# A decoder layer on one core: queries and keys projected without padding and spread by DMA, maxima by one transpose, scores by four or two heads, the projections' chain in two

## The chip, the core and the metric

The kernel runs on one core of a Trainium2 chip. A core has five engines that run their own instruction lists in order and meet only at semaphores: TensorE (PE in the profile; its weight loads are PEld), VectorE (DVE), ScalarE (ACT), GpSimd (POOL) and SyncE (SP), which here does nothing but issue DMAs. The metric is the time of one execution on the device in microseconds (us), the median of several runs.

## The reference

One layer, three sub-blocks, each followed by `x = layernorm(x + ...)`: a selective scan (a state-space block) whose state starts anew every 64 tokens, a cross attention of 16 heads of 16 columns to a given context, and a gated FFN in which each token belongs to one of eight experts by its position. Batch 32, 256 tokens, width 256, all in 32-bit floats.

```python
xc, res = jnp.split(x @ W_in.T + b_in, 2, axis=-1)          # 512 each
u = silu(conv(xc) + conv_b)                                  # causal, 3 taps
dlt, Bm, Cm = jnp.split(u @ W_x.T, [64, 80], axis=-1)
delta = softplus(dlt @ W_dt.T + b_dt)
dA = exp(einsum('bld,dn->bldn', delta, -exp(A_log)))
dBu = einsum('bld,bln,bld->bldn', delta, Bm, u)
carry = a * carry + bu ; y = einsum('bkdn,bkn->bkd', carry, c)
out1 = (y * silu(res)) @ W_out.T + b_out
...
q = proj(x, w_q, b_q) ; k = proj(ctx, w_k, b_k) ; v = proj(ctx, w_v, b_v)
attn = softmax(einsum('bhqd,bhkd->bhqk', q, k) / 4)
out2 = einsum('bhqk,bhkd->bhqd', attn, v) @ w_o.T + b_o
...
out3 = einsum('becf,efd->becd', silu(x @ w1) * (x @ w3), w2)
```

## The kernel before

**An order made by a planner.** `decoder_kernel` describes the work as chains, Python generators that yield the planned time and the engine of their next step. `in_order` (L78) keeps a planned clock per engine, always takes the chain that can go on first (ties by the chain's lag, the second argument in L1090 to L1104), and writes its instructions down. That order is final: on the chip each engine runs its list as written. The planner's durations are constants (`MM`, `EV`, `VE`, `GP` and numbers inside `spend`); a DMA counts as landed `LANDING` = 4.5 us after its step, and SP's own time is not counted, since no step spends on SP.

**Buffers.** PSUM has a ring of six banks for all products (`RING`, `take`, `done`, `bank`): a chain asks for n banks with a rank, and a step with a higher rank number waits while one with a lower asks.

**The scan** (`scan`, `decays`, `weighted`, `sums`). A batch has 16 steps of 32 channels by 16 states. SP loads delta and delta*u of step i+3, two DMAs that repeat rows over the states (`load_step`, L485), into one of four buffers; ScalarE makes the decays (four instructions, L519), in one of three buffers; VectorE multiplies (L544) and scans (L563), two of each; GpSimd multiplies by C (L580); after every four steps TensorE sums over the states (L594) and frees four of six state buffers.

**What feeds it** (`pre`, one chain for the whole of a batch): transpose x, project, convolve, `Silu` into `u` (L398, one buffer), then L408 on the product with `w_x`, the copy to DRAM (`bcd`, L422), delta through softplus on ScalarE and GpSimd, and two writes to DRAM (`dd`, L460 and L465) that the next batch's `load_step`s read. The small term of the softplus goes in two halves of two channel blocks (`lost`, L445 to L452).

**The attention** (`keys`, `attn`, `finish`). The host pads each head of `w_q`, `w_k` and their biases from 16 to 32 columns, so that four heads fill 128 partitions and each lies at a multiple of 32. The keys' bias holds 1.0 in the padded row 16 of each head. A padded projection is 512 columns: two `product`s of four matmuls (L626 to L638, L693 to L703), each copied with its bias by ScalarE (`biased`, L333) into `kT` and `qT`. Chain `keys` for batch b+1 starts after the last sum of batch b (`attended`), and `attn` takes one batch after the other.

In `attn` the first pass makes scores for four heads at a time (L715, four banks), and VectorE takes the maximum over keys (L731) into row 16 of each head's block of `mpad`. Eight 128x128 transposes (L739) turn `mpad`, and VectorE subtracts the result from `qT` (L742), which puts minus the maximum into row 16 of each head; its product with the keys' row of ones subtracts the maximum from the scores in the second pass. That pass makes the scores transposed, again four heads at a time, exponentiates them (`es`, L775) and multiplies by `v` with a column of ones (L751).

**The FFN** (`expert_unit`, `fetches`) runs in the gaps once a group of batches is stored, two units at a time at the end; the second set of units borrows the scan's buffers by tag.

All DMAs of the kernel are issued by SP. At the start it issues all weights, then 64 DMAs of `a_neg`, and `load_x(0)` last (L1088).

Of the kernel before, what the change touches and what calls it, by code (L numbers as in the profile page):

```python
# [95 lines left out]
def decoder_kernel(ctx: ExitStack, tc: tile.TileContext, a: dict, out: bass.AP):  # L96
# [54 lines left out]
    def row(name):  # L151
        t = wp.tile([P, D], F32, name=name)
        nc.sync.dma_start(t, a[name].partition_broadcast(P))
        return t

    w_in = weight("w_in", D, 2 * DI)
    b_in = column("b_in", 2 * NDC)
# [27 lines left out]
    b_out = row("b_out")  # L185
    w_k = weight("w_k", D, NG * P)
    b_k = column("b_k", NG)
    w_v = weight("w_v", D, D)
    w_out = weight("w_out", DI, D)
    w_q = weight("w_q", D, NG * P)  # L190
    b_q = column("b_q", NG)
    w_o = weight("w_o", D, D)
# [56 lines left out]

    mpad = keep.tile([P, 2, NG, P], F32, name="mpad")  # L250
    nc.gpsimd.memset(mpad, 0.0)

# [3 lines left out]
    def take(n, rank, t):  # L256
# [12 lines left out]
        del free[:n]  # L269

    def done(n, t):
        free.extend(n * [t])
# [12 lines left out]

    MM = 0.43
    EV = {1: 0.47, 2: 0.6, 4: 1.06}
# [49 lines left out]

    xs_at, xps, dds, sress, bcds, ygs, spread, silus = {}, {}, {}, {}, {}, {}, {}, []
    gated, stored = {}, []

    def exps():

        nc.scalar.preload_act_table_set("natural_log_exp_and_others")
        spend("ACT", 1.28)

    def pre(b):
# [50 lines left out]
        spend("ACT", 1.28)  # L397
        u = unit1.tile([P, NDC, L], F32, tag="u", name=f"u_{b}")  # L398
        for c2 in range(2):
            t = biased(u, AF.Silu, conv_b, pss[c2], c2)  # L400
            done(1, t)
        nc.scalar.activation(sres, sres, AF.Silu)
        spend("ACT", EV[4])
        sress[b] = sres
        while silus:
            silus.pop(0)()
        exps()
        yield from take(1, 3, t)  # L408
        ps = bank("ps_x")[:, :L]
# [34 lines left out]
        yield spend("ACT", EV[4]), "POOL"  # L444
        for h in range(2):  # L445
            cc = slice(2 * h, 2 * h + 2)

            lost = unit1.tile([P, 2, L], F32, tag="xT", name=f"lost_{b}")
            nc.gpsimd.tensor_scalar(lost, e[:, cc], 1.0, -1.0, op0=ALU.add, op1=ALU.add)
            nc.gpsimd.tensor_tensor(lost, e[:, cc], lost, ALU.subtract)  # L450
            nc.gpsimd.tensor_tensor(z[:, cc], z[:, cc], lost, ALU.add)
            yield spend("POOL", 3 * GP[2]), "POOL" if h == 0 else "ACT"  # L452
        nc.scalar.activation(e, e, AF.Ln, bias=1.0)
# [11 lines left out]
        nc.sync.dma_start(dds[b][1].rearrange("(c p) t -> p c t", p=P), u)  # L465
        spread[b] = t + 3.0

    def pres():
        for b in range(B):
            yield from pre(b)  # L470
        while silus:
            silus.pop(0)()
# [54 lines left out]
    def scan():  # L527
# [4 lines left out]
        for i in range(STEPS):  # L532
# [6 lines left out]
            for g in range(GB):  # L539

                if g:
                    yield t - 0.3 - MARGIN, "DVE"
                bu = ps_bu.tile([P, NQ, L], F32, tag="bu", name="bu")
                nc.vector.tensor_tensor(  # L544
                    bu, loads[i][:, 1, g].unsqueeze(1).to_broadcast([P, NQ, L]), b_bc, ALU.mult
                )
                t = spend("DVE", 0.66)
                if g == GB - 1:
                    del loads[i]
                    if k == NBLK - 1 and b + 1 < B:  # L550
                        yield t, "PE"
                        spread_b(b + 1)
                t -= 0.3 + MARGIN
                if g == 0:
                    yield lambda: (
                        max(t, decayed[i], min(h_free)) if i in decayed and h_free else None
                    ), "DVE"
                    h_free.sort()
                    del h_free[0]
                    h = hs[i] = hp.tile([P, GB, NQ, L], F32, tag="h", name="h")  # L560
                else:
                    yield t, "DVE"
                nc.vector.tensor_tensor_scan(  # L563
                    h[:, g].rearrange("p q t -> p (q t)"),
                    das_of[i][:, g].rearrange("p q t -> p (q t)"),
                    bu.rearrange("p q t -> p (q t)"),
                    0.0,
                    op0=ALU.mult,
                    op1=ALU.add,
                )  # L570
                t = spend("DVE", 1.17)
            del das_of[i]
# [10 lines left out]
    def sums():  # L583


        for i in range(NJ - 1, STEPS, NJ):
# [4 lines left out]
            for g in range(GB):  # L591
                for q in range(NQ):
                    for j in range(NJ):
# [8 lines left out]
                        )  # L602
            t = spend("PE", GB * NQ * MM + 0.3)
            h_free.extend(NJ * [t])
# [12 lines left out]
    kts, x1Ts, attended, oSs, ending = {}, {}, [], [], []  # L617

    def keys():

        for b in range(B):
# [3 lines left out]
            ctxT = cts.pop(b)  # L625
            kT = unit1.tile([P, NG, L], F32, tag="kT", name=f"kT_{b}")  # L626
            for g2 in range(2):
                yield from take(1, 4, t0)
                ps, t = product(
                    "ps_qk",  # L630
                    lambda j: [
                        w_k[:, k, (2 * g2 + j) * P : (2 * g2 + j + 1) * P] for k in range(2)
                    ],
                    lambda j: [ctxT[:, k, :] for k in range(2)],
                )
                yield t, "ACT"
                t = biased(kT, AF.Identity, b_k, ps, g2)
                done(1, t)  # L638
            yield from take(1, 4, t0)
# [8 lines left out]
            done(1, t)  # L648
            kts[b] = kT, t

# [38 lines left out]
    def attn(b):  # L689

        yield lambda: x1Ts[b][1] if b in x1Ts else None, "PE"
        x1, (x1T, tx) = x1s.pop(b), x1Ts[b]
        qT = unit1.tile([P, NG, L], F32, tag="qT", name=f"qT_{b}")  # L693
        for g2 in range(2):
            yield from take(1, 2, tx)
            ps, t = product(
                "ps_qk",
                lambda j: [w_q[:, k, (2 * g2 + j) * P : (2 * g2 + j + 1) * P] for k in range(2)],
                lambda j: [x1T[:, k, :] for k in range(2)],
            )  # L700
            yield t, "ACT"
            tq = biased(qT, AF.Identity, b_q, ps, g2)
            done(1, tq)  # L703
        del x1Ts[b]
        yield lambda: max(tq, kts[b][1]) if b in kts else None, "PE"
        kT = kts.pop(b)[0]

        def scores(g, left, right):


            ss = [bank("s").rearrange("p (t n) -> p t n", t=2) for _ in range(4)]
            for t in range(2):
                for j in range(4):
                    r = 32 * j
                    nc.tensor.matmul(  # L715
                        ss[j][:, t, :],
                        left[r : r + 32, g, t * P : (t + 1) * P],
                        right[r : r + 32, g, :],
                        start=True,
                        stop=True,  # L720
                    )
            return ss, spend("PE", 2 * MM + 0.5)


        t = tq
        for g in range(NG):
            yield from take(4, 2, tq)
            ss, ts = scores(g, qT, kT)
            for j, s in enumerate(ss):
                yield ts, "DVE"  # L730
                nc.vector.tensor_reduce(mpad[:, :, g, 32 * j + DK], s, AX.X, ALU.max)  # L731
                t = spend("DVE", VE[2])
                done(1, t)
        for g2 in range(2):
            yield from take(1, 2, t)
            ps = bank("ps_m").rearrange("p (j t n) -> p j t n", j=2, t=2)
            for j in range(2):
                for n in range(2):
                    nc.tensor.transpose(ps[:, j, n, :], mpad[:, n, 2 * g2 + j, :], ident)  # L739
            yield spend("PE", 0.6), "DVE"  # L740
            q2 = qT[:, 2 * g2 : 2 * g2 + 2, :]
            nc.vector.tensor_tensor(q2, q2, ps.rearrange("p j t n -> p j (t n)"), ALU.subtract)  # L742
            tq = spend("DVE", VE[2])
            done(1, tq)

        def attend(g, ess):

            oT = bank("ps_oT")[:, :L]
            for k in range(2):
                for j in range(4):  # L750
# [8 lines left out]
                    )  # L759
            return oT, spend("PE", 2 * MM + 0.3)  # L760

        last, oS, te = None, None, 0.0
        for g in range(NG + 1):
            if g < NG:
                yield from take(4, 2, tq)
                ss, ts = scores(g, kT, qT)
            if g:
                yield from take(1, 0, te)
                oT, to = attend(g - 1, last)
            if g < NG:  # L770
                ess = []
                for s in ss:
# [5 lines left out]
                    done(1, te)  # L778
                last = ess
            else:  # L780
                attended.append(to)
# [84 lines left out]
    class Buffers:  # L866
# [18 lines left out]
        def h(self, u, n):  # L885

            m = 2 * L // n
            if self.own:
                t = unit1.tile([P, 3 * m, n], F32, tag="h_ff", name=f"h_{u}")
                return [t[:, b * m : b * m + m, :] for b in range(3)]  # L890
            return [
                unit1.tile([P, m, n], F32, tag=tag, name=f"h_{tag}_{u}")
                for tag in ("u", "delta", "e")
            ]
# [182 lines left out]
    def units(bufs):  # L1077
# [19 lines left out]
        Chain(finishes(), -3.0),  # L1097
        Chain(pres(), 1.0),
        Chain(keys(), 1.5),
    ]  # L1100
# [69 lines left out]
```

## Time and profile before

| | us |
|---|---|
| median of 3 runs (lowest, highest) | 3283.39 (3279.27, 3285.63) |
| the profiled execution | 3283.71 |
| its span, first to last instruction | 3282.0 |

| engine | busy us | share of the span | instructions |
|---|---|---|---|
| PE | 2697.9 | 82% | 18436 |
| PEld | 1907.2 | 58% | 18436 |
| DVE | 2584.0 | 79% | 3511 |
| ACT | 1970.8 | 60% | 4211 |
| POOL | 1857.3 | 57% | 1241 |

The mean granted TensorE clock is 0.897, and DMA queue 1, which is SP's, holds the 16 DMA engines busy 47.8% of the span. The first scan runs at 119.8 us, the last loads of the scan are issued at 2962.7, and from 3100 to 3282 VectorE works 33 us of 182: FFN is left there. A row of the profile that names one line of a helper (L327 is in `product`, L333 in `biased`) is told apart by its tiles. In a row of the groups, the columns are line, engine, operation, out<-in, shapes and count, then busy time and mean ns of one, then the idle time of the engine just before and what ended it. In a list of waits they are total us, number, and the longest.

### The profile page before, as it was taken

The numbers are of one execution on the slowest core, as the hardware profiler recorded it, in microseconds if no ns is written. First come the engines' busy times: TensorE is split into PE (matmuls) and PEld (weight loads), VectorE is DVE, ScalarE is ACT, GpSimd is POOL, SyncE is SP. The second block draws the span as 40 slices with busy tenths as digits, with TensorE's granted clock in tenths as the row PEclk, the third lists the DMA queues.
The fourth block names the chain that finished last, engine by engine and source line by source line (L and its number), as shares of the span: only waits on it lengthen the run. The fifth ranks groups of instructions, "written<-read, shape, count | busy, mean of one in ns | idle before, by whom it ended". The sixth has DMA issues, their size and how long they took to land.

```text
span 3282.0 us, 52502 instructions
## 1 busy us (share of the span) xinstructions
PE 2697.9 (82%) x18436; PEld 1907.2 (58%) x18436; DVE 2584.0 (79%) x3511; ACT 1970.8 (60%) x4211; POOL 1857.3 (57%) x1241
## 2 busy tenths in 40 slices
PE   2568787878888988888888898888788888898987
PEld 1345555556556666566555566556566556565776
DVE  0598989898988988888989878989878898884211
ACT  0556666666666766676666656766656666764411
POOL 1576666666766656665656556665656666642000
PEclk9678888888889899999998899899899889899998
DMA  3354444444445555444544544445445544454474
GB/s 89 110 149 115 139 120 138 126 138 127 132 129 151 158 145 147 140 134 133 154 137 138 145 140 147 137 137 140 128 142 148 148 139 137 130 152 132 130 225 140
DMA packets 310681, 455.00 MB, mean 139 GB/s; under 512 B 37969, under 2 KB 158033, under 8 KB 310417
## 3 DMA queue, kind: packets, MB, share of 16 engines
q1 hardware_dynamic: 310416, 451.64, 47.8%
q8 instruction: 146, 2.39, 0.3%
q14 instruction: 119, 0.97, 0.1%
HBM read 400.67 MB, written 50.86 MB: 138 GB/s over the span
## 4 chain that ended last, share of the span: by engine, by line
DVE 44%; PE 27%; POOL 8%; ACT 8%; DMA 6%; issue 5%; SPq 2%; DVEq 1%; ACTq 0%; POOLq 0%
DVE h L563 23%; DVE bu L544 12%; PE ps_h L978 7%; PE s L715 4%; DVE mpad L731 4%; POOL h L580 3%; PE ps_down L1058 3%; PE ps_in L327 3%; PE y L594 3%; PE ps_oT L751 2%; ACT da L519 2%; ACT es L775 2%; PE ps_conv L327 2%; DMA ld<-dd 1%; PE ps_qk L327 1%
## 5 line engine op out<-in xcount | busy, mean ns | idle before, releaser
L580 POOL TENSOR_TENSOR h<-h,c_bc 128x1024 f32<-128x1024 f32 x512 | 1207.8, 2360 | 935.0 <-DVE h L563 810.8
L563 DVE TENSOR_TENSOR_SCAN h<-da,bu 128x512 f32<-128x512 f32 x1024 | 1248.4, 1219 | 116.8 <-PE y L594 11.0
L519 ACT ACTIVATE da<-ld,a_neg 128x252 f32<-128x252 f32 x2048 | 889.9, 506 | 395.6 <-DVE h L563 289.8
L544 DVE TENSOR_TENSOR bu<-ld,b_bc 128x512 f32<-128x512 f32 x1024 | 709.6, 693 | 95.4 <-PE b_bc L503 68.1
L594 PE MATMUL y<-h,sel_y 128*32 128x256 f32 x4096 | 334.1, 440 | 85.6 <-POOL h L580 73.4
L731 DVE TENSOR_REDUCE mpad<-s 128x2 f32<-128x512 f32 x512 | 315.5, 681 | 111.3 <-PE s L715 110.8
L775 ACT ACTIVATE es<-s 128x512 f32<-128x512 f32 x512 | 263.9, 601 | 191.6 <-PE ps_oT L751 144.9
L978 PE MATMUL ps_h<-x2T,w 128*128 128x256 f32 (+3 forms) x1440 | 331.0, 377 | 41.3 <-ACT x2T L966 36.2
L715 PE MATMUL s<-kT,qT 32*128 32x256 f32 x2048 | 248.9, 475 | 101.9 <-DVE mpad L731 63.3
L978 PEld LDWEIGHTS ps_h<-x2T,w 128*128 128x128 f32 (+1 forms) x1440 | 241.5, 193 | 110.7 <-ACT x2T L966 40.3
L594 PEld LDWEIGHTS y<-h,sel_y 128*32 128x32 f32 x4096 | 150.3, 124 | 253.8 <-POOL h L580 119.6
L327 PE MATMUL ps_in<-xT,w_in 128*128 128x256 f32 x1024 | 268.9, 415 | 13.5 <-ACT xT L352 12.0
L715 PEld LDWEIGHTS s<-kT,qT 32*128 32x128 f32 x2048 | 155.4, 218 | 189.2 <-DVE mpad L731 98.8
L327 PEld LDWEIGHTS ps_in<-xT,w_in 128*128 128x128 f32 x1024 | 205.5, 208 | 68.9 <-issue 12.8
L715 PE MATMUL s<-qT,kT 32*128 32x256 f32 x2048 | 180.1, 438 | 39.4 <-DVE qT L742 23.4
L301 POOL TENSOR_SCALAR ln_rstd<-ln_mv 128x2 f32<-128x2 f32 x96 | 22.0, 230 | 309.6 <-DVE ln_mv L298 305.0
L327 PE MATMUL ps_conv<-xpad,taps 128*128 128x256 f32 x768 | 182.6, 388 | 0.0
L751 PE MATMUL ps_oT<-es,v 128*32 128x256 f32 x2048 | 149.1, 410 | 40.6 <-DVE h L1040 13.1
L1058 PE MATMUL ps_down<-w,h 128*128 128x256 f32 (+1 forms) x624 | 164.2, 409 | 16.4 <-DVE h L1040 7.5
L715 PEld LDWEIGHTS s<-qT,kT 32*128 32x128 f32 x2048 | 112.4, 202 | 96.1 <-issue 25.6
L327 PEld LDWEIGHTS ps_conv<-xpad,taps 128*128 128x128 f32 x768 | 146.5, 194 | 25.0 <-issue 3.1
L327 PE MATMUL ps_out<-w_out,yg 128*128 128x256 f32 x512 | 133.2, 419 | 28.5 <-ACT es L775 20.9
(124 smaller groups left out, 3701.4 us busy)
## 6 DMA issues: line engine op xcount, KB each, us to landing
ld<-dd SPq DMA_DIRECT2D x1024, 256.0 KB
w<-in_w SPq DMA_DIRECT2D x120, 352.0 KB
x<-in_x SPq DMA_DIRECT2D x64, 256.0 KB
dd<-delta SPq DMA_DIRECT2D x32, 512.0 KB
dd<-u SPq DMA_DIRECT2D x32, 512.0 KB
w13y<-in_w SPq DMA_DIRECT2D x40, 352.0 KB
w<-in_w SPq DMA_DIRECT2D x30, 384.0 KB
ctxT<-in_ctxT SPq DMA_DIRECT2D x32, 256.0 KB
```

The lines of the kernel that those rows point to most:

```text
L327: nc.tensor.matmul(ps[:, j, :], l, r, start=(k == 0), stop=(k == len(terms) - 1))
L519: nc.scalar.activation(da[:, g, q].rearrange("p (k t) -> p k t", t=CHUNK)[:, :, 1:], loads[i][:, 0, g].rearrange("p (k t) -> p k t", t=CHU ...
L544: nc.vector.tensor_tensor(bu, loads[i][:, 1, g].unsqueeze(1).to_broadcast([P, NQ, L]), b_bc, ALU.mult)
L563: nc.vector.tensor_tensor_scan(h[:, g].rearrange("p q t -> p (q t)"), das_of[i][:, g].rearrange("p q t -> p (q t)"), bu.rearrange("p q t - ...
L580: nc.gpsimd.tensor_tensor(hs[i], hs[i], c_bc, ALU.mult)
L594: nc.tensor.matmul(y[32 * j : 32 * j + 32, :], sel_y[:, g, :], hs[i - NJ + 1 + j][:, g, q, :], start=(g == 0 and q == 0), stop=(g == GB - ...
L715: nc.tensor.matmul(ss[j][:, t, :], left[r : r + 32, g, t * P : (t + 1) * P], right[r : r + 32, g, :], start=True, stop=True,)
L731: nc.vector.tensor_reduce(mpad[:, :, g, 32 * j + DK], s, AX.X, ALU.max)
L751: nc.tensor.matmul(oT[32 * j : 32 * j + 32, :], v[:, k, 4 * g + j, :], ess[j][:, k, :], start=(k == 0), stop=(k == 1), tile_position=(0, 3 ...
L775: nc.scalar.activation(es, s, AF.Exp, scale=1.0 / DK**0.5)
L978: nc.tensor.matmul(ps[:m, i, :], w_tiles[u, which, e][k][:, f * P : f * P + m], right, start=(k == 0), stop=(k == 1),)
L1058: nc.tensor.matmul(po[:, j, :], h[i // m_in][:m, i % m_in, cols], w_tiles[u, "w2", e][f // 3][:m, f % 3, :], start=(i == terms[0]), stop=( ...
```

## The change

It changes five things.

1. **Projections.** `heads(n)` loads only the 16 real columns of each head from the padded weights (two DMAs each) and the biases head by head (16 DMAs each). A projection is then one `product` and one pair of biased copies into a dense tile `k_flat` or `q_flat`, and `spread_heads` copies each head by a DMA on SP to its place at a multiple of 32 in `kT` or `qT`, 16 DMAs of 16 partitions by 256. `kT` and `qT` are now tiles that are kept; `kT` is set to 1.0 once, which leaves the row of ones.
2. **Maxima.** They go into a dense tile `tops` of 2 x 16 columns, one transpose turns it, ScalarE copies it with its sign changed into `rows`, and 32 DMAs on SP put each head's and half's 128 values into row 16 of the head in `qT`. The subtraction on VectorE goes.
3. **Scores.** A step takes two banks, and two more if `more` finds them free; the matmuls contract over 16 rows (first pass) or 17 (second) and not 32.
4. **The projections' chain** ends after `Silu`; a new chain `steps()` does the rest (`sizes`), with two buffers for `u`, and a batch may start while fewer than two are waiting. The small term goes channel block by channel block, with a tile of its own.
5. **Planner figures:** `MM` 0.47, 0.71 and 1.23 for the scan's two operations, 0.1 to 0.2 in place of 0.3 to 0.5 after groups of matmuls.

```diff
+    def heads(n):
+        w = wp.tile([P, 2, D], F32, name="w_" + n)
+        src = a["w_" + n].rearrange("(k p) (h c) -> p k h c", p=P, c=32)
+        for k in range(2):
+            dst = w[:, k].rearrange("p (h c) -> p h c", c=DK)
+            nc.sync.dma_start(dst, src[:, k, :, :DK])
+        bias = wp.tile([P, 2], F32, name="b_" + n)
+        for h in range(H):
+            r = DK * (h % 8)
+            j = 32 * (h % 4)
+            src = a["b_" + n][j : j + DK, h // 4 : h // 4 + 1]
+            nc.sync.dma_start(bias[r : r + DK, h // 8 : h // 8 + 1], src)
+        return w, bias
...
-    w_k = weight("w_k", D, NG * P)
-    b_k = column("b_k", NG)
+    w_k, b_k = heads("k")
...
-    mpad = keep.tile([P, 2, NG, P], F32, name="mpad")
-    nc.gpsimd.memset(mpad, 0.0)
+    kT = keep.tile([P, NG, L], F32, name="kT")
+    nc.gpsimd.memset(kT, 1.0)
+    qT = keep.tile([P, NG, L], F32, name="qT")
+    tops = keep.tile([P, 2, H], F32, name="tops")
...
+    def more(n):
+        if sum(t <= clock.now for t in free) < n or len(asking) > 1 and min(asking) < 2:
+            return 0
+        free.sort()
+        del free[:n]
+        return n
...
-        u = unit1.tile([P, NDC, L], F32, tag="u", name=f"u_{b}")
+        u = unit2.tile([P, NDC, L], F32, tag="u", name=f"u_{b}")
...
+    def sizes(b):
+        yield lambda: us[b][1] if b in us else None, "PE"
+        u, t = us[b]
         yield from take(1, 3, t)
...
-        for h in range(2):
-            cc = slice(2 * h, 2 * h + 2)
-            lost = unit1.tile([P, 2, L], F32, tag="xT", name=f"lost_{b}")
+        for c in range(NDC):
+            lost = unit1.tile([P, L], F32, tag="lost", name=f"lost_{b}")
...
     def pres():
         for b in range(B):
+            yield lambda: 0.0 if len(us) < 2 else None, "PE"
             yield from pre(b)
...
+    def spread_heads(dst, flat):
+        for g in range(NG):
+            for j in range(4):
+                h = 4 * g + j
+                r = DK * (h % 8)
+                nc.sync.dma_start(dst[32 * j : 32 * j + DK, g, :], flat[r : r + DK, h // 8, :])
...
+            flat = unit1.tile([P, 2, L], F32, tag="k_flat", name=f"k_flat_{b}")
+            tk = biased(flat, AF.Identity, b_k, ps, 0)
+            done(1, tk)
+            yield tk, "SP"
+            spread_heads(kT, flat)
+            tk = clock.now + LANDING
...
+        h = 0
+        while h < H:
+            yield from take(2, 2, tq)
+            n = 2 + more(2 if h % 4 == 0 else 0)
+            ss, ts = scores(range(h, h + n), qT, kT, DK)
+            for s in ss:
                 yield ts, "DVE"
-                nc.vector.tensor_reduce(mpad[:, :, g, 32 * j + DK], s, AX.X, ALU.max)
+                nc.vector.tensor_reduce(tops[:, :, h], s, AX.X, ALU.max)
                 t = spend("DVE", VE[2])
                 done(1, t)
+                h += 1
+        yield from take(1, 2, t)
+        ps = bank("ps_m")[: 2 * H, :P]
+        nc.tensor.transpose(ps, tops.rearrange("p t h -> p (t h)"), ident)
+        yield spend("PE", 0.2), "ACT"
+        rows = unit1.tile([2 * H, P], F32, tag="rows", name=f"rows_{b}")
+        nc.scalar.activation(rows, ps, AF.Identity, scale=-1.0)
+        t = spend("ACT", 0.35)
+        done(1, t)
+        yield t, "SP"
+        for t in range(2):
+            for g in range(NG):
+                for j in range(4):
+                    h = t * H + 4 * g + j
+                    r = 32 * j + DK
+                    nc.sync.dma_start(qT[r : r + 1, g, t * P : (t + 1) * P], rows[h : h + 1, :])
+        tq = clock.now + LANDING
...
-                yield from take(4, 2, tq)
-                ss, ts = scores(g, kT, qT)
+            while g < NG and len(ess) < 4:
+                yield from take(2, 2, tq)
+                n = 2 + more(0 if ess else 2)
+                h = 4 * g + len(ess)
+                ss, ts = scores(range(h, h + n), kT, qT, DK + 1)
+                if g and not ess:
+                    yield from take(1, 0, te)
+                    oT, to = attend(g - 1, last)
...
+        Chain(steps(), 0.5),
```

The second set of FFN units takes its buffer tagged `u` from the pool with two buffers.

## The prediction

> **What bounds the kernel now.** I read the chain of waits first, then the busy time of four batches in the steady part, then the durations by line, and last SP's own queue, because the change gives SP most of its new work.
>
> ```profile
> DVE 44%; PE 27%; POOL 8%; ACT 8%; DMA 6%; issue 5%; SPq 2%; DVEq 1%; ACTq 0%; POOLq 0%
> ```
> ```profile
> 1540.00:1631.00 91.00, 80.30 (x565) 55.08 (x564) 83.60 (x113) 60.03 (x133) 60.29 (x40) 0.94 0.52 148
> ...
> sum 357.00, PE 302.18 PEld 209.56 DVE 312.91 ACT 234.40 POOL 225.45; mean PE 75.55 PEld 52.39 DVE 78.23 ACT 58.60 POOL 56.36
> ```
>
> The second fence holds the windows of four successive batches (each from one query projection to the next; columns: window, length, busy PE, PEld, DVE, ACT, POOL, clock, DMA share, GB/s). A batch takes 357/4 = 89.3 us, of which VectorE works 78.2, TensorE 75.6, ScalarE 58.6, GpSimd 56.4. Nothing is full. VectorE is nearest, and its 11 us of idle time per batch come from an order that is fixed at build time: each engine runs its own list in order, so an engine that waits for one late input holds everything behind it. The loop has about 31 such batches, plus a start and a tail.
>
> ```profile
> L742 DVE TENSOR_TENSOR qT<-qT,ps_m 128x512 f32<-128x512 f32 x64 | 41.9, 674 | 5.1 <-PE ps_m L739 5.0
> L739 PE MATMUL ps_m<-ident,mpad 128*128 128x128 f32 x256 | 45.2, 302 | 22.0 <-DVE mpad L731 22.0
> L327 PE MATMUL ps_qk<-x1T,w_q 128*128 128x256 f32 x512 | 126.1, 391 | 0.0
> L327 PE MATMUL ps_qk<-ctxT,w_k 128*128 128x256 f32 x512 | 125.3, 389 | 7.2 <-DMA ctxT<-in_ctxT 4.7 <-DVE yg L610 2.5
> L333 ACT ACTIVATE qT<-ps_qk,b_q 128x256 f32<-128x256 f32 x128 | 53.2, 468 | 17.6 <-PE ps_qk L327 17.5
> ```
>
> **What is removed.** VectorE: the two subtractions L742, 2 x 0.674 = 1.35 us a batch. TensorE: half of both projections, (126.1 + 125.3)/2/32 = 3.9 us, and seven of eight transposes, 45.2/32 x 7/8 = 1.2 us. ScalarE: four biased copies of 0.469 less one small negating copy (nearest row oS, 0.383): 1.5 us. Only VectorE's 1.35 us lie on the engine nearest to its limit.
>
> **Scores by two.** One group of four heads is 16 instructions and holds PE 1.08 us in the chain of waits. For a group of two (8 instructions) the trace has no row: between half of that (no loss) and the same 1.08 us, if two row groups run as long as four. With all eight groups of a batch split that is 0 to +8.6 us of PE; I take a quarter, +2.2, since half of them should find four banks and the size of a split lies between. PE nets 3.9 + 1.2 - 2.2 = 2.9 us less. In return a step needs two free PSUM banks of six, not four. Of VectorE's 11 us of idle time I credit 2 us a batch to both together (bounds 0 and 5).
>
> **Off the path.** The split of the small-term tile makes 12 GpSimd instructions of 256 columns out of 6 of 512. From 2351 ns at 1024 columns and 1269 at 512 a tensor_tensor costs about 723 at 256, the tensor_scalar (1936) about 1057 with the same fixed part: 4 x 2.50 - 2 x 4.47 = +1.1 us of GpSimd, hidden in its 33 idle us; 1.1 us if that cover goes. Cutting the projections' chain in two and the new planner figures (0.47, 0.71, 1.23) issue no other instructions; they move the order. The second half carries five SP issues of its own (bcd, delta, c_bc twice, u), which can now stand behind a block of new copies, and the next batch's loads wait for the last of them; in the batch above that u went out at 1569.89 and the next load at 1579.55, so some 10 us hide it, less than a block of 16. I put 0 on all this (bounds -1 and +1 us a batch).
>
> **What is added: DMA issues on SP.** Each batch gets 16 copies for keys, 16 for queries (16 partitions x 1 KB each) and 32 of one row (512 B). All go on SP's queue, which also issues the loads of the scan.
>
> ```profile
> L422 SPq DMA_DIRECT2D bcd<-xp x32: 335/524/1106, 91.8 to 2836.6; - x32
> L845 SPq DMA_DIRECT2D x2d<-x x32: 366/383/1084, 302.9 to 3092.1; - x32
> L181 SPq DMA_DIRECT2D a_neg<-in_a_log x64: 584/597/600, 7.9 to 48.3; - x64
> ```
> ```profile
> 7.89 40.98 SPq L181 DMA_DIRECT2D a_neg<-in_a_log  x64
> 50.44 0.34 SPq L148 DMA_DIRECT2D b_k<-in_b_k  x1
> ```
>
> The durations (first fence; least/median/most, ns) and SP's timeline at the start show that an issue costs about the same whatever it moves: 383 ns for 256 KB, 524 for 16 KB, 597 for 0.5 KB, where 64 in a row took 40.98 us, 0.64 each with the gap. The nearest row to the new copies is bcd (16 partitions x 1 KB): I take 0.50 with the gap, bounds 0.38 and 0.64. So 64 x 0.50 = 32 us of SP a batch (24 to 41), in blocks of 8, 8 and 16 us.
>
> [...]
>
> ```profile
> SPq L485 <- DVE bu L544: 1376.6, 438, 8.2
> SPq L195 <- DMA w_k<-in_w_k: 0.7, 1, 0.7
> SPq L171 <- DMA w_in<-in_w_in: 1.1, 1, 1.1
> ```
> ```profile
> ACT da L519 <- DMA ld<-dd: 97.1, 71, 4.7
> ```
> ```profile
> 1580.22 3.64 DMA ld<-dd
> ```
>
> The first line: SP issues the scan's load the moment its buffer comes free (438 times), so a block in front of it delays it one for one. The next two are odd: b_v has nothing to do with w_k, nor the bias row of w_dt with w_in; in each case the load waited for is the one eight issues earlier. No more than eight copies are in flight. At 0.50 each that binds only if a copy needs over 4 us to land, and 64 a_neg copies ran at 0.64 without such a wait, so they land within 5.1 us: an upper price of 0.64 again.
>
> Now the block of 32 rows, 16 us. The load for step i+3 is due when step i-1 is done. In a stretch of pure scanning a step takes 2 x 2.07 = 4.15 us (VectorE's timeline, 1584 to 1600, just where the rows will fall), so it has 3 x 4.15 = 12.4 us, less 3.6 to land (the piece of the chain above) and 0.9 for the first decays: 7.9 us of slack. On average the first load hits the block 2.1 us in: 16 - 2.1 - 7.9 = 6 us late. At the batch's mean step (89.3/16 = 5.6) the slack is 12.3 and the stall about 1. Between the two: **+3.5 us** a batch (0 to 8). ScalarE's queue holds the decays ahead of exponentials and copies, so these are late next. The blocks of 8 us fit into the slack when apart and not when back to back (then 6 late): **+1** (0 to 5).
>
> ```profile
> 1586.15 0.60 PE L739 MATMUL ps_m<-ident,mpad 128*128 128x128 f32 x4
> ...
> 1591.00 1.15 PE L715 MATMUL s<-qT,kT 32*128 32x256 f32 x16
> ```
>
> The second wait is PE's. Before, transposed scores began 4.9 us after the last transpose. Now the first pair needs rows of both halves of the tokens, the 18th of 32 issues: 18 x 0.50 + 3.6 = 12.6 us after the copy, while the planner puts these scores 4.5 us after. (That a reader waits only for its own part of a tile shows at the start, where the product with w_x began at 88.00 while ScalarE wrote the second half of u from 88.20.) For up to 8 us PE's queue stands, with sums, projections and FFN products behind it; scanning goes on until its six state buffers are used up. PE has 14 idle us a batch, and the stretch is the same one that the late loads already cost: **+1** (0 to 8).
>
> **Start and tail.** Start: weights by 2 + 2 issues and biases by 16 + 16 in place of 4, so 32 more, all ahead of the first x, and nothing runs before x. At 0.34 (b_k) 11 us, at 0.64 (a_neg) 20: +16. Tail: after the last scan the attention of the last batch has little beside it; its three landings are longer by about 8 (rows) and 4: +12 (0 to 20).
>
> **Sum.** -1.35 - 2 + 3.5 + 1 + 1 = +2.15 us a batch, x 31 = +67; +16 + 12 = **+95**. The profiled execution took 3283.71 us (span 3282.0 and 1.7 around it), the median of the runs is 3283.39, so no correction: 3283.7 + 95 = **3379**, say 3380.
>
> **Rivals.** (1) *Faster: the blocks stay in SP's slack.* SP waited 1376.6 us for buffers, over 40 us a batch, so 32 us can fit if they fall in gaps with wide steps. Then 3.35 us a batch are kept: 3283.7 - 3.35 x 31 + 16 + 5 = 3201. For it: fewer banks per step, shorter queues on PE and ScalarE. Against it: 16 us in one block where steps are 4.15 us. It decides if an issue costs under about 0.33 us in the block (10.5 us, within 7.9 + 2.1). (2) *The attention becomes the bound.* One batch's attention starts only after the one before, and keys only after the last sums: over batches 2 to 29 the medians in PE's timeline are 28 us from the end of one to the first scores of the next, 20 for the first pass, 6 for the maxima, 36 for the second: a closed ring of 90 us with no gap. The keys' spread adds about 4 net of the halved product, the rows 8 net: if the planner cannot fill the 28 us more tightly, +10 a batch, 3283.7 + 310 + 28 = 3622. Against: those 28 us hold low-priority waiting. (3) *It does not do what it says:* four banks are hardly ever free, so scores always go by two. At full price PE then has 75.6 - 5.1 + 8.6 = 79 us a batch, still under 89; with 2 us of it felt, 3380 + 62 = 3442, inside the forecast's side. (4) *No change:* the terms cancel within 0.2%, about what this kernel's runs can tell from nothing.
>
> **How the numbers follow.** Forecast with (3) 0.53, own range 3300 to 3500; faster 0.29; attention-bound 0.14; no change 0.04. So faster 0.29, slower 0.53 + 0.14 = 0.67. For 8 in 10 the range reaches down to the middle of the faster case, 3205, and up to 3600.
>
> **What would show it.** Right: SP's issues of the one-row copies at 0.4 to 0.6 us; ScalarE's decays waiting for the scan's loads far over 97.1 us; PE waiting at the transposed scores for a DMA, 5 us and more; first x load some 16 us later. Wrong on size: those waits small because the planner put the copies in gaps. Wrong altogether: VectorE's share above 87% in the steady batches and a batch of 86 us or less.

## The result and the profile after

The changed kernel took 3834.06 us (median of 4 runs, 3817.41 to 3841.49), the kernel before 3282.77 us: a ratio of 1.167, 95% interval 1.163 to 1.172. It is slower by 551 us, 17.2 us for each of 32 batches. The forecast had the sign and about a sixth of the size; the measured time lies above its range.

Where the time stands: the first scan starts at 138.0 us and not at 119.8, the stretch from first to last scan is 3402.8 us and not 2861.8 (+541), and what follows the last scan starts is 285 us and not 300. So nearly all of it is lost in the loop.

The page of the kernel after, the chain of waits:

```profile
PE 29%; SPq 11%; DMA 7%; DVE 6%; ACT 4%; POOL 3%; issue 2%; DVEq 0%; ACTq 0%; POOLq 0%
SPq L794 9%; PE ps_h L1032 7%; PE s L759 6%; DMA ld<-dd 4%; PE y L629 3%; PE ps_down L1112 3%; DVE h L598 3%; PE ps_in L351 2%; ACT da L554 2%; DVE bu L579 2%; SPq L660 1%; PE ps_out L351 1%; POOL h L615 1%; PE ps_oT L802 1%; PE ps_qk L351 1%
```

Before, SP's own queue had 2% of the chain; now it has 11%, 9% of it on one line, L794, the one-row copies. These shares add up to 62% only, where those of before added up to the whole: the chain could not be followed back to the start. Of the part that was followed, VectorE has about a tenth (6 of 62), where it had 44% before: it no longer sets the pace. The costliest groups of VectorE and its neighbours, with idle time and what ended it at the right:

```profile
L598 DVE TENSOR_TENSOR_SCAN h<-da,bu 128x512 f32<-128x512 f32 x1024 | 1247.7, 1218 | 225.3 <-PE y L629 127.7
L554 ACT ACTIVATE da<-ld,a_neg 128x252 f32<-128x252 f32 x2048 | 874.6, 502 | 735.5 <-DMA ld<-dd 558.2
...
L759 PE MATMUL s<-qT,kT 17*128 17x256 f32 x2048 | 374.4, 541 | 405.6 <-DMA qT<-rows 337.5
```

The scan itself costs what it did (1248 us). ScalarE's wait for the scan's loads grew from 97.1 to 558.2 us, and TensorE now waits 337.5 us for the one-row copies before the second pass. VectorE, which does the scan, mostly waits for neither of them itself. Its waits for TensorE's sums over the states, before and after:

```profile
DVE yg L610 <- PE y L594: 29.6, 24, 3.1
DVE h L563 <- PE y L594: 11.0, 6, 2.2
```
```profile
DVE yg L645 <- PE y L629: 175.7, 53, 13.2
DVE h L598 <- PE y L629: 127.7, 16, 11.0
```

One block of copies, in the timelines of SP, ScalarE, TensorE and VectorE:

```profile
1563.69 1.17 SPq L520 DMA_DIRECT2D ld<-dd  x2
1564.95 20.74 SPq L794 DMA_DIRECT2D qT<-rows  x32
1585.79 2.48 SPq L520 DMA_DIRECT2D ld<-dd  x4
```
```profile
1569.12 0.90 ACT L554 ACTIVATE da<-ld,a_neg 128x252 f32<-128x252 f32 x2 [1.03 <-DVE h L598]
1580.02 2.07 ACT L827 ACTIVATE es<-s 128x512 f32<-128x512 f32 x4 [10.00 <-PE s L759]
1589.30 1.69 ACT L554 ACTIVATE da<-ld,a_neg 128x252 f32<-128x252 f32 x4 [7.21 <-DMA ld<-dd]
```
```profile
1576.91 3.90 PE L759 MATMUL s<-qT,kT 17*128 17x256 f32 x16 [7.02 <-DMA qT<-rows]
```
```profile
1584.48 0.42 DVE L645 TENSOR_TENSOR yg<-y,sres 128x256 f32<-128x256 f32 x1 [8.37 <-PE y L629]
```

The block takes 20.74 us, 0.65 an issue. For that long no load of the scan goes out; two steps' loads follow at once, the first has landed by 1589.3, and ScalarE, which makes the decays, has stood twice: 10.0 us for scores that hang on the rows, 7.2 for the load. TensorE has stood 7.0 us for the rows, and VectorE 8.4 for sums that TensorE has in its list behind those scores. Two suspects, late loads and late scores, lie in the same 20 us. The experiments had to part them.

At the start the first x goes out at 75.69 us in SP's timeline, before at 55.83: 19.9 us later.

### The profile page after: what moved, and what is told of

Same layout as the page of the kernel before. It is cut to its first block, busy times and chain, and to the rows that moved or that the text cites. A ratio compares the mean times of both kernels' runs of the same rounds, so it can differ in the third digit from the quotient of the medians.

```text
span 3826.2 us, 54098 instructions
## 1 busy us (share of the span) xinstructions
PE 2892.6 (76%) x17700; PEld 1989.8 (52%) x17700; DVE 2557.6 (67%) x3447; ACT 1895.0 (50%) x4103; POOL 1887.7 (49%) x1433
## 4 chain that ended last, share of the span: by engine, by line
PE 29%; SPq 11%; DMA 7%; DVE 6%; ACT 4%; POOL 3%; issue 2%; DVEq 0%; ACTq 0%; POOLq 0%
SPq L794 9%; PE ps_h L1032 7%; PE s L759 6%; DMA ld<-dd 4%; PE y L629 3%; PE ps_down L1112 3%; DVE h L598 3%; PE ps_in L351 2%; ACT da L554 2%; DVE bu L579 2%; SPq L660 1%; PE ps_out L351 1%; POOL h L615 1%; PE ps_oT L802 1%; PE ps_qk L351 1%
## 5 line engine op out<-in xcount | busy, mean ns | idle before, releaser
L554 ACT ACTIVATE da<-ld,a_neg 128x252 f32<-128x252 f32 x2048 | 874.6, 502 | 735.5 <-DMA ld<-dd 558.2
L579 DVE TENSOR_TENSOR bu<-ld,b_bc 128x512 f32<-128x512 f32 x1024 | 709.9, 693 | 152.9 <-DMA ld<-dd 82.9
L759 PE MATMUL s<-qT,kT 17*128 17x256 f32 x2048 | 374.4, 541 | 405.6 <-DMA qT<-rows 337.5
L759 PEld LDWEIGHTS s<-qT,kT 17*128 17x128 f32 x2048 | 244.3, 248 | 520.8 <-issue 396.5
L776 DVE TENSOR_REDUCE tops<-s 128x2 f32<-128x512 f32 x512 | 319.8, 682 | 214.7 <-PE s L759 214.0
L1032 PE MATMUL ps_h<-x2T,w 128*128 128x256 f32 (+3 forms) x1440 | 382.1, 415 | 25.8 <-ACT xT L376 12.2
L629 PE MATMUL y<-h,sel_y 128*32 128x256 f32 x4096 | 345.7, 471 | 65.3 <-POOL h L615 53.8
L759 PE MATMUL s<-kT,qT 16*128 16x256 f32 x2048 | 263.6, 482 | 145.8 <-DMA qT<-q_flat 78.8
L759 PEld LDWEIGHTS s<-kT,qT 16*128 16x128 f32 x2048 | 169.5, 224 | 227.7 <-issue 124.7
L802 PE MATMUL ps_oT<-es,v 128*32 128x256 f32 x2048 | 182.1, 466 | 5.5 <-DVE h L1094 2.2
L478 POOL TENSOR_SCALAR lost<-ez 128x256 f32<-128x256 f32 x128 | 137.7, 1076 | 87.6 <-ACT ez L473 84.9
L702 POOL TENSOR_TENSOR x<-x,b_out 128x512 f32<-128x512 f32 x32 | 40.5, 1266 | 282.1 <-DMA x<-in_x 251.1
L645 DVE TENSOR_TENSOR yg<-y,sres 128x256 f32<-128x256 f32 x128 | 52.9, 413 | 175.8 <-PE y L629 175.7
```

Source lines behind the costliest of these rows:

```text
L554: nc.scalar.activation(da[:, g, q].rearrange("p (k t) -> p k t", t=CHUNK)[:, :, 1:], loads[i][:, 0, g].rearrange("p (k t) -> p k t", t=CHU ...
L579: nc.vector.tensor_tensor(bu, loads[i][:, 1, g].unsqueeze(1).to_broadcast([P, NQ, L]), b_bc, ALU.mult)
L629: nc.tensor.matmul(y[32 * j : 32 * j + 32, :], sel_y[:, g, :], hs[i - NJ + 1 + j][:, g, q, :], start=(g == 0 and q == 0), stop=(g == GB - ...
L759: nc.tensor.matmul(s[:, t, :], left[r : r + n, g, t * P : (t + 1) * P], right[r : r + n, g, :], start=True, stop=True,)
L776: nc.vector.tensor_reduce(tops[:, :, h], s, AX.X, ALU.max)
L802: nc.tensor.matmul(oT[32 * j : 32 * j + 32, :], v[:, k, 4 * g + j, :], ess[j][:, k, :], start=(k == 0), stop=(k == 1), tile_position=(0, 3 ...
```

## The experiments

Theory A: the 64 issues occupy SP, the loads of the scan stand behind them, and this makes the loss. Rivals are named in the expectations. Times stand against the kernel before on the same chip: 3283.9 us for the parts of the change and the told kernel, 3283.7 for the next two and the merged kernel's first run, 3283.5 for the idle kernels in a fixed order, 3281.4 for the other two idle kernels, the merged kernel in rounds and the shorter start. All are single runs except those with an interval; four runs of the merged kernel lie up to 27 us apart, seven of the kernel before 6, so a difference of some 20 us in a single run is weak.

**Parts of the change, one at a time.** Without any of the new copies, and with one buffer for `u`, so that the projections' chain is in effect not cut:

```diff
-    w_k, b_k = heads("k")
+    w_k = weight("w_k", D, NG * P)
+    b_k = column("b_k", NG)
...
-        rows = unit1.tile([2 * H, P], F32, tag="rows", name=f"rows_{b}")
+        for g2 in range(2):
+            ps = bank("ps_m").rearrange("p (j t n) -> p j t n", j=2, t=2)
...
-        u = unit2.tile([P, NDC, L], F32, tag="u", name=f"u_{b}")
+        u = unit1.tile([P, NDC, L], F32, tag="u", name=f"u_{b}")
```

> The kernel after without its two new sets of copies: padded projections and the maxima by eight transposes and a subtraction are back, scores by two or four and the new planner figures stay; one buffer for u for want of space, so the projections' chain is in effect not cut. Theory A (the 64 copies' issue time on SP delays the scan's loads and the transposed scores): 3200 to 3330 us, ScalarE's wait for the loads near 97 us. Rival B (scores by two and the new figures made a worse order, the copies are incidental): 3500 us or more.

Measured: 3301.52 us, ScalarE's wait for loads 63.5 us. Rival B falls: with scores by two or four and the new planner figures the kernel is 18 us slower than before, and the other 532 come with the copies and the cut chain. (That the cut chain makes no such loss is seen below, where the merged kernel has it and is faster.)

With the one-row copies only (padded projections put back):

> Padded projections are back, so no spreading; the 32 one-row copies of the maxima stay, chain cut. Theory A: the block of 32 issues (20.7 us) is the larger half of the cost, since it is over the loads' slack and holds the second pass: 3560 to 3700 us. Rival C (the two blocks of 16 do it, because they often come back to back just when the next attention has to start): under 3450 us.

Measured: 3661.16 us. With the spreading only (the maxima by eight transposes; a mask clears row 16 of each head in the same VectorE instruction that subtracts):

```diff
+            nc.vector.scalar_tensor_tensor(
+                q2, q2, real[:, 0:1], ps.rearrange("p j t n -> p j (t n)"), op0=ALU.mult, op1=ALU.subtract
+            )
```

> Dense projections with 16 + 16 spreading copies stay, the maxima go by eight transposes and a subtraction with a mask; no one-row copies, chain cut. Theory A: each block of 10 us is near the loads' slack and costs when the two meet: 3350 to 3520 us, PE's long wait before the transposed scores gone. Rival C: 3600 us or more.

Measured: 3472.41 us. Over the kernel without copies the rows cost 359.6 us and the spreading 170.9, together 530.5; the whole change costs 532.5 over it. Rival C falls: the rows are two thirds of it. That the two add up holds for the totals only. From the first scan to the last the rows cost 198 us (3117.2 against 2918.9) and the spreading 119 (3038.0), the whole change 484; the kernel with rows only loses 161 us more behind its last scan (419 us against 258).

**Is the order wrong, or SP full?** The planner is told SP's time; no instruction is added or taken away:

```diff
         spread_heads(qT, flat)
-        tq = clock.now + LANDING
+        tq = spend("SP", 16 * 0.64) + 3.5
...
-        lds_at[i] = clock.now + LANDING
+        lds_at[i] = spend("SP", 2 * 0.6) + LANDING - 1.2
```

> The kernel after with the same instructions, but the planner is told that SP takes 0.64 us per copy (also 0.6 for a scan load, 0.5 to 0.75 for weights and c_bc) and that copies land 3.5 us after their last issue. Theory A in the form 'SP is occupied': the loads stay behind the blocks, PE's wait for the rows shrinks: 3650 to 3800 us. Rival D (the order is wrong only because the planner puts scores 4.5 us after a block that takes 20): 3300 to 3500 us.

Measured: 3967.20 us, above both. In its list of waits:

```profile
ACT da L555 <- DMA ld<-dd: 614.9, 111, 22.7
...
PE s L760 <- DMA qT<-rows: 59.2, 12, 13.7
```

TensorE's wait for the rows is gone but for 59 us (337 before it), as planned, and the kernel is 133 us slower. Rival D falls: telling the planner repairs nothing. The run does not show that TensorE's wait was free. The rows land no sooner; the planner only puts other work in front of the scores, which now start 23.7 us (mean) after the first pass and not 17.3. The order of everything else changed too: TensorE's wait for GpSimd before the sums rose from 53.8 to 390.7 us, the loads' wait grew, and 118 of the 133 us lie behind the last scan.

**The same issues, but behind the loads.** Groups of four copies in a chain of their own that gives way to any load due on SP:

```diff
+    def copies():
+        for _ in range(B * 4 * NG):
+            yield lambda: jobs[0][0] if jobs else None, "SP"
+            _, what, copy = jobs.pop(0)
+            copy()
+            landed[what] = spend("SP", 4 * 0.64) + 3.5
...
+        Chain(copies(), 100.0),
```

> The told kernel (e4) with the same 64 issues, but in groups of four that form a chain of their own and stand back behind any load that is due on SP. Loads then wait for at most one group of 2.6 us. Theory A in the form 'blocks delay the loads': ScalarE's wait for loads falls from 615 to under 200 us and the time from 3967 to 3450 to 3650 us. Rival E (ring): the wait falls but the time stays at 3800 us or more, since the copies land no sooner.

Measured: 3612.50 us, 355 less than the told kernel, ScalarE's wait down from 614.9 to 277.6. Within the forecast in time, not in the wait (under 200 was expected). It doesn't reach the kernel before: in TensorE's timeline the median time from the end of one batch's attention to the next one's first scores is now 35.5 us, against 28.2 before, so the copies that give way come late for the attention. That is rival E in part: with 64 issues either the loads or the attention waits. What follows the last scan is 403 us in both kernels; all of the gain lies in the loop.

**The rows on another queue.** GpSimd issues the 32, all else equal:

```diff
-                    nc.sync.dma_start(qT[r : r + 1, g, t * P : (t + 1) * P], rows[h : h + 1, :])
+                    nc.gpsimd.dma_start(qT[r : r + 1, g, t * P : (t + 1) * P], rows[h : h + 1, :])
```

> The kernel after with the 32 one-row copies issued by GpSimd's queue and not by SP's; the rest is the same. The loads then see only the two blocks of 16. Theory A in the form 'the block delays the loads': 3450 to 3650 us, ScalarE's wait for loads at most that of the spread-only kernel (500 us). Rival E (the time until the rows have landed, whoever issues them): 3750 us or more. GpSimd's own price per issue has no row so far; at 1 us it is 32 us of its some 50 idle us a batch.

Measured: 3842.12 us, as the kernel after: a miss for theory A as it stood, and what rival E forecast. Four lines of its waits:

```profile
ACT da L554 <- DMA ld<-dd: 348.3, 83, 17.1
...
PE s L759 <- DMA qT<-rows: 319.4, 42, 15.9
...
PEld y L629 <- POOL h L615: 218.8, 92, 21.3
...
PE y L629 <- POOL h L615: 166.1, 70, 20.8
```

ScalarE's wait for loads fell (558.2 to 348.3), and the time did not; TensorE's wait for the rows is nearly what it was (337.5). So either the loads' wait was not what set the time, or the block costs on GpSimd what it had cost on SP: it now stands in front of GpSimd's multiplication by C, and TensorE's sums wait up to 21 us for that (the last two lines were 70.6 and 53.8 us after the change). A GpSimd issue costs 0.484 us (median), so the block is some 15.5 us long there, an estimate from 32 of them. This run speaks for rival E and does not prove it.

**Idle copies in the kernel before.** The cleanest test of what late loads alone can do: SP issues one-row copies that nobody waits for, at the place where the maxima are done.

```diff
+        yield t, "SP"
+        for h in range(32):
+            nc.sync.dma_start(idle[h : h + 1, :], mpad[h : h + 1, 0, 0, :])
```

> The kernel before, unchanged but for 32 one-row copies (512 B) that SP issues when a batch's maxima are done, from a row of mpad to a tile that nobody reads. No instruction waits for them; they only occupy SP for some 20.7 us a batch. Theory A with the prediction's slack formula at 0.645 us an issue: 20.7 less 2.1 to 2.8 less 7.9 to 12.3 is a stall of 5.6 to 10.7 us a batch, 3460 to 3620 us. Rival E (it is the late maxima that cost, not the loads behind the block): 3283 to 3330 us.

> The same with 16 copies a batch, 10.3 us of SP. Theory A: by the same formula 0 to 0.3 us a batch, so a threshold and no line: 3283 to 3330 us. Rival F (every issue on SP costs in proportion, slack or no slack): half of the rise of the 32.

Measured: 3724.72 us with 32, 3419.42 with 16, against 3281.4. That is +443 and +138: much for copies without a reader. Both times lie above what the slack formula gave. The added step on SP had let the planner order the other engines anew, so two more kernels issue the copies without a step, and all engines but SP keep the order of before:

> As the kernel with 32 idle copies, but TensorE, VectorE, ScalarE and GpSimd have exactly the instructions of before in exactly the order of before (the step on SP had let the planner order some of them anew); SP alone has 32 more issues a batch, right after the last maximum is planned. Theory A (SP's occupied time alone): 3600 to 3800 us, like the 3725 of the other. Rival G (the new order did it): under 3400 us.

> The same with 8 copies a batch, 5.2 us of SP. From 16 to 32 copies the time rose 305 us, which is 0.60 us an issue and batch, so nearly the whole issue; drawn back, the rise starts at about 9. Theory A with a threshold: 3270 to 3310 us. Rival F (proportional from the first issue): 3283 + 8/32 of the rise of 32, about 3390 us.

Measured: 3761.50 us with 32 (+478) and 3304.90 with 8 (+21). Rivals G and F fall. SP's and ScalarE's timelines in the kernel with 32:

```profile
1496.97 21.02 SPq L735 DMA_DIRECT2D idle<-mpad  x32
1518.10 0.53 SPq L465 DMA_DIRECT2D dd<-u  x1
1518.73 1.43 SPq L920 DMA_DIRECT2D w<-in_w  x2
1520.21 3.28 SPq L485 DMA_DIRECT2D ld<-dd  x4
```
```profile
1501.74 2.06 ACT L775 ACTIVATE es<-s 128x512 f32<-128x512 f32 x4 [0.85 <-PE s L715]
1526.08 1.69 ACT L519 ACTIVATE da<-ld,a_neg 128x252 f32<-128x252 f32 x4 [22.28 <-DMA ld<-dd]
```

ScalarE stands 22.3 us behind one block, since its list has the decays next: from 1503.8 to 1526.1 us it runs nothing. Over the kernel its wait is:

```profile
L519 ACT ACTIVATE da<-ld,a_neg 128x252 f32<-128x252 f32 x2048 | 884.4, 505 | 909.8 <-DMA ld<-dd 647.8 <-DVE h L563 254.6 <-DVE mpad L731 3.4
```

It rose from 97.1 to 647.8, by 551 us, and the time by 478. Per batch the blocks of about 5.2, 10.4 and 20.8 us cost 0.67, 4.3 and 14.9 us: about 6 us are free, and past them each us of block costs a us (10.4 - 4.3 = 6.1; 20.8 - 14.9 = 5.9). (The 16 copies were timed in the new order only.)

How ScalarE's stand reaches VectorE is in the same run's list of waits:

```profile
PE ps_oT L751 <- ACT xpad L374: 242.0, 15, 21.8
DVE bu L544 <- PE b_bc L503: 236.4, 17, 56.6
DVE bu L544 <- DMA ld<-dd: 229.1, 22, 16.7
```

Before, these were 7.3, 68.1 and nothing. VectorE stands 229.1 us for the loads themselves, 7.2 a batch. The rest comes round by two engines: ScalarE's copies (`xpad`) are in its list behind the late decays, TensorE stands for them, and its products come late: VectorE's wait for the spread of B (`b_bc`) grew by 168 us, for the sums by 76. With 16 copies VectorE stands only 13.8 us for loads, so nearly all of the 138 us came that way.

**Where each kernel loses it.** The attention is a closed ring: a batch starts when the one before has ended. Its phases on TensorE, from the starts and ends of the scores (`s`) and of the last product with `v` (`ps_oT`), means over 31 batches in us:

| | before | after | rows on GpSimd | 32 idle copies, fixed order | merged (below) |
|---|---|---|---|---|---|
| end of the last batch to first pass | 30.4 | 26.8 | 26.9 | 30.6 | 23.4 |
| first pass | 18.9 | 25.7 | 25.9 | 18.6 | 21.7 |
| first pass to second: the maxima | 6.8 | 17.3 | 17.4 | 6.8 | 9.6 |
| second pass | 34.6 | 38.3 | 38.2 | 49.9 | 33.8 |
| the ring | 90.7 | 108.1 | 108.4 | 105.9 | 88.5 |

The kernel after loses 10.5 us at the maxima, where the rows have to land, and 6.8 in the first pass; the idle copies lose 15.3 in the second pass, where the late loads hit, and nothing at the maxima. So late loads alone are dear, but they are not where the kernel after loses its time. There the trace points to the rows: TensorE stands for them in each of the 32 batches (3.6 to 13.4 us), and with the loads freed of the block of rows (GpSimd) the ring is as it was.

**Fewer issues, same bytes.** If SP's occupied time is the root of both waits, a block of 5 us should cost next to nothing and leave the change's savings:

```diff
+        for g in range(2):
+            for j in range(4):
+                r = DK * (4 * g + j)
+                dst_ = dst[32 * j : 32 * j + DK].rearrange("p (o g) t -> p g o t", g=2)[:, g]
+                nc.sync.dma_start(dst_, flat[r : r + DK])
...
+        for t in range(2):
+            for g in range(NG):
+                h = t * H + 4 * g
+                nc.sync.dma_start(qT[DK : P : 32, g, t * P : (t + 1) * P], rows[h : h + 4, :])
```

> The kernel after with the same bytes moved in fewer issues: 8 per spread (both halves of a head's rows in one copy) and 8 for the maxima (four rows to four partitions 32 apart), so 24 issues a batch and not 64; planner untouched. Theory A (issue time on SP): a block is 5 us and fits the loads' slack of 8 us: 3250 to 3400 us, ScalarE's wait for loads under 150 us. Rival E (the three landings lengthen the attention's ring, however few the issues): 3550 us or more.

> The merged kernel again (24 issues a batch), timed in rounds. Theory A: 3200 to 3220 us, ratio to before 0.975 to 0.981.

Measured: 3211.13 us, faster than was forecast, and 3207.16 in rounds (3194.85 to 3221.91; ratio to before 0.977, 0.974 to 0.981). One source change in two helpers turns a loss of 551 us into a gain of 74. The block of the maxima in SP's timeline and two lines of the page's groups:

```profile
1595.70 1.16 SPq L520 DMA_DIRECT2D ld<-dd  x2
1596.96 4.43 SPq L792 DMA_DIRECT2D qT<-rows  x8
1601.48 8.41 SPq L520 DMA_DIRECT2D ld<-dd  x6
```
```profile
L554 ACT ACTIVATE da<-ld,a_neg 128x252 f32<-128x252 f32 x2048 | 879.7, 504 | 333.0 <-DVE h L598 156.6
...
L759 PE MATMUL s<-qT,kT 17*128 17x256 f32 x2048 | 281.5, 482 | 134.9 <-DMA qT<-rows 93.6
```

ScalarE's idle time is again ended mostly by VectorE, not by loads, and TensorE's wait for the rows fell from 337.5 to 93.6 us; four rows of 512 B in one copy take SP 4.43/8 = 0.55 us, no more than one row did (0.65).

**A shorter start.** The merged kernel with 8 copies for each bias and `a_neg` loaded behind the first x:

```diff
-        for h in range(H):
-            r = DK * (h % 8)
+        for h in range(H // 2):
+            src = a["b_" + n][32 * (h % 4) : 32 * (h % 4) + DK].rearrange("p (o g) -> p g o", g=2)
+            nc.sync.dma_start(bias[DK * h : DK * h + DK, :], src[:, h // 4])
```

> The merged kernel with a shorter start: the biases in 8 copies each and not 16, and the 64 copies of a_neg issued after the first x (its exponential and sign change on ScalarE before the first decays). Some 30 to 50 us less before the first product; if the start lies on the path, 3160 to 3190 us, ratio to before 0.962 to 0.972. Rival: something else at the start, such as GpSimd's set-up or the first context, ends last: no change from the merged kernel.

Measured: 3203.21 us (ratio 0.977, 0.974 to 0.980), no more than can be told from the merged kernel. The first x goes out at 28.6 us, but the 64 copies of `a_neg` then hold SP until 70.6, in front of the first context and weights, and the first scan starts at 133.3 us against 138.6. The wait changed places; the rival holds.

## Why the prediction was wrong, point by point

- **What is removed: right in kind.** Merged, with blocks that fit, the loop from first to last scan is 2795.1 us against 2861.8, -2.1 us a batch in spite of 24 copies; the prediction credited -3.35. That its faster case of 3201 is so near the measured 3207 is in part luck: it had -104 for the loop and +21 for start and tail, measured are -67 and -10. (One slip in its sums moves nothing: from 2351 and 1269 ns a tensor_tensor of 256 columns comes to 728 ns, not 723.)
- **The price of an issue: at its upper bound.** 0.50 was taken, 0.65 measured (20.74 us for 32), so blocks of 10.3, 10.3 and 20.7 us in place of 8, 8 and 16. The row it was like was a_neg, from which the bound came, not bcd.
- **The step that failed: TensorE's wait for the rows, "+1 (0 to 8)".** The wait itself was worked out rightly: the same sum at 0.65 an issue gives 18 x 0.65 + 3.6 - 4.5 = 10.8 us, and TensorE stood 337.5/32 = 10.5 a batch. What failed is the overlap that made it nearly free: "PE has 14 idle us a batch, and the stretch is the same one that the late loads already cost". TensorE's list behind the scores holds the sums; VectorE's waits for them rose by 263 us in all, and the ring is longer by 10.5 us a batch at just that place. VectorE's own wait for the loads, which was to be the larger cost, is 82.9 us, 55.7 of it a single wait before the first scan. Rows alone cost 359.6/32 = 11.2 us a batch, where the sum had 3.5 + 1.
- **"+3.5 us a batch (0 to 8)" for the loads behind the rows: a second gap, by what it left out.** The idle copies put a price on late loads alone, 14.9 us a batch. For VectorE's own stand the prediction's formula holds: at 0.65 an issue it gives 5.6 to 10.7 us, measured are 7.2 with 32 copies, and with 16 it gives 0 to 0.3, measured 0.4. But the prediction counted only to the moment at which VectorE lacks its step, three steps on. ScalarE stands sooner (in the idle block above from 1503.8 us, VectorE from 1514.0), and of its copies and exponentials behind the decays the prediction says "these are late next" and gives no price. That way costs the other half, 7.7 us a batch with 32 copies, and nearly all of it with 16. It is why only about 6 us of a block are free; what sets just that number was not tried.
- **The two blocks of 16: "+1 (0 to 5)".** The spreading costs 170.9/32 = 5.3 us a batch, over the upper end. The timeline after shows them back to back or one scan load apart in most batches, because queries and keys become ready together.
- **The cut chain's own issues, "I put 0".** In the kernel with 32 idle copies a block stands in front of the write of u in some batches, and the next batch's loads wait for both. That cost is inside the 14.9 and was not parted from it.
- **Start: +16, measured +19.9 for the first x and +18 for the first scan. Tail: +12, measured -15:** the part after the last scan became shorter.
- **Rival 2 (the attention's ring, 3622 us) was the nearest picture.** It put 8 us net on the rows and 4 on the keys' spread, +10 a batch in all. Measured are a ring of 108.1 us in place of 90.7, 10.5 of it at the maxima and 6.8 in the first pass. It got 0.14.

What is shown and what is not: that the number of issues on SP makes the loss is shown by the merged kernel, which moves the same bytes. That late rows are the wait that counts in the kernel after is read from its trace and from the run with the rows on GpSimd, where GpSimd's own queue also had the block. No run has late rows without any other engine's queue being held, so how much the rows alone would cost stays open.

## What to carry to other kernels

In this kernel a DMA's price on the queue that issues it was paid per issue and not per byte (medians: 0.38 us for 256 KB before, 0.59 for 0.5 KB after): count issues, and look at what else the queue has to send in that time. Ask of a block of small copies who waits for its last copy and what stands in that engine's list behind the wait, and who waits for the prefetch behind the block and what stands behind that: here the second alone was enough to lose 15%. About 6 us of block were free, and beyond that it cost one for one; merging copies brought the blocks below it. An idle-copy kernel, the kernel before with copies that nobody reads, prices the second of these alone. Taking away one of two waits that overlap need not move the time.

## What the runs showed of the hardware that was not expected

The granted TensorE clock fell where time was lost: 0.897 before, 0.806 after, 0.803 in the told kernel; the merged kernel, the fastest of these, had 0.882. With the same TensorE instructions, the kernel with 32 idle copies was granted 0.844 and was busy 2754.8 us with them, not 2697.9. From before to after TensorE's busy share fell with the clock (82% of the span, then 76%), but the two do not go together everywhere: the merged kernel, with 83%, was granted less than the kernel before (in the stretch from 1000 to 2800 us it was busy for 1584.9 us at 0.91, the kernel before for 1534.6 at 0.92). No run shows what sets the clock, and whether the lower clock added to the time was not tried.

SP's issue of one 512-byte row took 0.587 us (median, kernel after), and of four such rows to four partitions 32 apart 0.497 (merged kernel): the larger copy was the cheaper one.
